# Zero rows, loads of x, clearings and the rows of h rearranged in the first epoch of a graph kernel

## The chip, the cores and the metric

The kernel runs on one core of one Trainium2 chip. The time is device microseconds of the whole launch, the median of three runs. The core has five engines with instruction queues of their own: PE (matrix multiply), DVE (vector), ACT (scalar functions), POOL (GpSimd) and SP, which here does nothing but issue DMAs. ACT and POOL issue some DMAs too. Each engine takes its instructions in program order, and an instruction that must wait holds up all those behind it on its engine.

## The reference

The input is 12,500 nodes with 128 features each and 400,000 edges. An edge e has a source node `src[e]`, a target `dst[e]` (the edges are sorted by `dst`), 20 numbers `f[e]` and a weight `w[e]`. Cut to what matters:

```python
h   = relu(layernorm(x)) @ W_in2f.T
Wij = (smu(f_ij @ W_f1.T + b_f1) @ W_f2.T + b_f2) * w[:, None]
agg = segment_sum(h[dst] * Wij, src)        # 12500 x 128
out = x + smu(agg @ W_o1.T + b_o1) @ W_o2.T + b_o2
```

`smu` is a smooth rectifier made of a linear part and an erf part. So each edge fetches a row of h by its sorted index `dst`, multiplies it by a filter that is computed from its 20 numbers, and adds the product into the row `src` of `agg`.

## The kernel before

**Tiles.** Nodes are taken in NB = 98 blocks of 128. Edges are taken in tiles of 128: four tiles make a *group* (512 edges, NG = 782 groups), and two groups make a *sup* (391 of them). Sups are divided into nine *epochs* (`PARTS`): 59 sups, or 118 groups, make the first epoch.

**What a group does.** `hide`, `bend` and `smooth` compute the hidden layer (PE `pu`, ACT `ge`, DVE `sm`); `weigh` multiplies by the second matrix (PE `pw`). `gather` fetches rows of h: a window of 128 rows of `h_dram`, loaded by `window` as `hw`, times a one-hot matrix `oh` (PE `ph`), copied by ACT to `hg`. `mix` multiplies the two (DVE `mt`, L577), `turn` transposes the product (PE `pt`), and `send` scales by the edge's weight (ACT `ms`, L597) and issues four scatters from POOL (L600), one for each tile of 128 edges. A scatter writes its 128 message rows into the DRAM buffer of the epoch, `buf`, sorted coarsely by the node block of `src`. The slot of each row is counted by `bins`, `count`, `read` and `number` (DVE `po`, `co`; PE `pc`; ACT `jk`, L495; DVE `ix`, L504). `ms` has six buffers. While epoch k is being scattered, epoch k-1's buffer is read back and summed into `agg` on PE (L655). This doesn't happen yet in the first epoch.

**SP's queue.** At the start of every second group `load(s + 3)` asks for `f`, for `rbc` (from `rel_dram`) and for the window `hw` (L405, L407, L416) of the sup three ahead. Slots of `buf` that may stay unwritten must hold zeros. `clear` writes zeros there (L167), from SP. In the first epoch the clearings of its own buffer are spread over the first 38 groups (`BY - 6`), while scatters already go to other slots of the same buffer. From group `BY` on, a scatter is ordered behind these clearings; a count taken at `BY` verifies that this was allowed. From `BY` to the end of the epoch the next epoch's buffer is cleared.

**The first epoch's other work.** The tile `agg` first holds x (as `x_sb`). `late_loads` asks for x past the first four blocks (`HEAD`) from POOL's queue (L381, L382), then for `w_sb` and small weights. `others` is a generator of small steps, which `step()` spreads evenly: it is called three times in each group and takes the next step when one is due. The steps are: for chunks c = 1 to 6 of the edge indices (512 tiles each), nine steps of `head_of(c)` (`fetched` asks for `dst` and `src` from SP, L301 and L302; `based` begins on DVE with `base_i`, L305; `written` stores `rel_dram`, L328), with the mean and variance of one block of x (`stats`, L180 and L181) after each; then the other `stats`, two blocks a step; `deviations`; and then 24 units of rows of h, each of four blocks and of six steps. The six steps of `rows_of_h` are `normed` (DVE, L191), `turned` (PE, L197), `cut` (ACT, L200), `product` (PE, L205), `first_part` (ACT L208, DVE L209) and `other_parts` (ACT L212, DVE L213, store from SP, L214). h is stored in three bf16 parts. In this order each step needs the result of the step taken just before it. `zeroed` (L731 to L733) writes zeros to the rows of `h_dram` behind the last block.

The order on PE, DVE, ACT and SP is the program's own order; there is no planner.

Of the kernel before, what the change touches and what calls it, by code (L numbers as in the profile page):

```python
# [9 lines left out]
F32 = mybir.dt.float32  # L10
# [9 lines left out]
P = 128  # L20
# [19 lines left out]
def gnn_kernel(  # L40
# [129 lines left out]


    HEAD = 4
    BY = 44
    x_sb = agg.rearrange("p (b d) -> p b d", d=D)
    mv = const.tile([P, NB, 2], F32, name="mv")
    rstd = const.tile([P, NB], F32, name="rstd")
# [84 lines left out]
    with tc.tile_pool(name="ld", bufs=4) as ld, \  # L261
# [14 lines left out]
        def fill(i):  # L276
            nc.vector.memset(fbufs[i], 1.0)

        hs = edge.tile([P, GRP, 3, D], BF, name="hs", bufs=1)
        early = eps_of[0][1] + 3  # L280

        def bank(name):
# [2 lines left out]
        def head_of(c):  # L285


            a, n = c * CH, min(CH, NT - c * CH)
            s0, m = a // SUP, (n + SUP - 1) // SUP
            rw = rowp.tile([P, ROWS, ROW], F32, name="rw").rearrange("p q r -> p (q r)")  # L290
            di, si, rel = rw[:, 0:n].bitcast(I32), rw[:, CH:CH + n].bitcast(I32), rw[:, 2 * CH:2 * CH + n]
            if c:
                rb = hs[:, :, 0, :]
            else:
                rb = edge.tile([P, SUP * P], BF, name="oh", bufs=3)[:, :CH].rearrange("p (j e) -> p j e", e=P)
            base_f = edge.tile([1, CH // SUP], F32, name="base_f")
            cells = [(j * P, min(P, n - j * P)) for j in range((n + P - 1) // P)]
            kept = [None]

            def fetched():  # L300
                nc.sync.dma_start(di, dst_col[:, a:a + n])  # L301
                nc.sync.dma_start(si, src_col[:, a:a + n])  # L302

            def based():
                nc.vector.tensor_copy(base_i[:, s0:s0 + m], di[0:1, 0:n:SUP])  # L305
                nc.vector.tensor_copy(base_f[:, :m], base_i[:, s0:s0 + m])
                nc.vector.tensor_copy(rel, di)

            def spread():
                pb = kept[0] = bank("pb")  # L310
                flat = pb.rearrange("p j e -> p (j e)")[:, :m * SUP].rearrange("p (s t) -> p s t", t=SUP)
                nc.tensor.matmul(flat, ones1, base_f[:, :m].unsqueeze(2).to_broadcast([1, m, SUP]),
                                 start=True, stop=True)

            def lowered():
                nc.vector.tensor_sub(rel, rel, kept[0].rearrange("p j e -> p (j e)")[:, :n])

            def turned():
                pd = kept[0] = bank("pd")
                for j, (o, w) in enumerate(cells):  # L320
                    nc.tensor.transpose(pd[:w, j, :], rel[:, o:o + w], ident)

            def written():
                w = cells[-1][1]
                whole = len(cells) - (w < P)
                if whole:
                    nc.scalar.activation(rb[:, :whole], kept[0][:, :whole], AF.Copy)
                    nc.sync.dma_start(rel_dram[0, a * P:(a + whole * P) * P].rearrange("(c t e) -> t c e", t=P, e=P),  # L328
                                      rb[:, :whole])
                if w < P:  # L330
                    nc.scalar.activation(rb[:w, whole], kept[0][:w, whole], AF.Copy)
                    nc.sync.dma_start(rel_dram[0, (a + whole * P) * P:(a + n) * P].rearrange("(t e) -> t e", e=P),
                                      rb[:w, whole])

            def limits():
                nc.vector.tensor_reduce(lh[:, 0, c:c + 1], rel, op=ALU.min, axis=AX.X)
                nc.vector.tensor_reduce(lh[:, 1, c:c + 1], rel, op=ALU.max, axis=AX.X)

            def bounded():
                most = edge.tile([1, 1], F32, name="most")  # L340
                nc.vector.tensor_reduce(most, base_f[:, :early], op=ALU.max, axis=AX.X)
# [22 lines left out]
        nc.scalar.dma_start(w_f2, w_f2_t)  # L364
        nc.scalar.dma_start(b2, b_f2.rearrange("o p -> p o"))
        nc.scalar.dma_start(w_sb[:, 0:CH], w_col[:, 0:CH])
        for i in range(NF):
            fill(i)
        nc.vector.memset(zero, 0.0)
# [4 lines left out]
        def late_loads():  # L374

            nc.vector.memset(x_sb[:, NB - 1, :], 0.0)
            parts_of_x = chunks(NB - 1 - HEAD, 31)
            for a, n in parts_of_x:
                nc.vector.memset(x_sb[:, HEAD + a, 0:1], 0.0)
            for a, n in parts_of_x:  # L380
                nc.gpsimd.dma_start(x_sb[:, HEAD + a:HEAD + a + n, :], bin_rows(x, HEAD + a, n))  # L381
            nc.gpsimd.dma_start(x_sb[:LASTB, NB - 1, :], x[(NB - 1) * P:N, :])  # L382
            nc.vector.memset(w_sb[:, CH:CH + 1], 0.0)
            nc.gpsimd.dma_start(w_sb[:, CH:NT], w_col[:, CH:NT])
            nc.gpsimd.dma_start(w_o1, w_o1_t)
# [309 lines left out]
            stats(edge, b)  # L695
        deviations(0, HEAD)
        rw = rowp.tile([P, ROWS, ROW], F32, name="rw")
        for step in rows_of_h(0, HEAD, *[rw[:, j * GRP:(j + 1) * GRP, 0:P] for j in range(3)], hs, bank):
            step()
        for s in range(3):  # L700
            window(s)
# [25 lines left out]
        cleared = at_first = done = 0  # L727
        work = []

        def zeroed():  # L730
            zr = edge.tile([P, 3 * D], BF, name="zr", bufs=1)  # L731
            nc.vector.memset(zr, 0.0)
            nc.sync.dma_start(h_dram[NB * P:N + WIN, :], zr[:N + WIN - NB * P, :])  # L733

        def output_bias():

            nc.vector.tensor_scalar(w_o2, w_o2, GC, None, op0=ALU.mult)
# [3 lines left out]
            nc.tensor.matmul(pb1, b1w, w_o2, start=True, stop=True)  # L741
            nc.vector.tensor_add(bo2, bo2, pb1)

        def others():
            yield one["limits"]
            yield zeroed
            left = list(range(HEAD, NB))
            for c in range(1, NC):
                it = head_of(c)
                for name in ("fetched", "based", "spread", "lowered", "turned", "written", "binned", "placed", "limits"):  # L750
                    yield it[name]
                    if left:
                        yield lambda b=left.pop(0): stats(edge, b)
            while left:
                two, left = left[:2], left[2:]
                yield lambda two=two: [stats(edge, b) for b in two]
            yield lambda: deviations(HEAD, NB)
            for b, n in chunks(NB - HEAD, GRP):
                rw = rowp.tile([P, ROWS, ROW], F32, name="rw")
                four = [rw[:, j * GRP:(j + 1) * GRP, 0:P] for j in range(3)]  # L760
                yield from rows_of_h(HEAD + b, n, *four, hs, bank)
            yield output_bias

        COUNT = 2 + 18 * (NC - 1) + (NB - HEAD - 9 * (NC - 1) + 1) // 2 + 1 + 6 * -(-(NB - HEAD) // GRP) + 1
        h_steps = others()
        taken_steps = slot = 0

        def step():

            nonlocal taken_steps, slot  # L770
            slot += 1
            while taken_steps < COUNT and taken_steps * 3 * (eps_of[0][1] * PER - 12) < slot * COUNT:
                next(h_steps)()
                taken_steps += 1

        for g in range(NG):
# [7 lines left out]
                cleared = 0  # L784
            if g < BY:

                while at_first < min(len(cleans) - 1, -(-(g + 1) * (len(cleans) - 1) // (BY - 6))):
                    apart(clear(0, at_first, nc.sync), "filled", "cleared")
                    at_first += 1
            elif k + 1 < EPOCHS:  # L790
# [34 lines left out]
            bins(g + 3)  # L825
            parts(k - 1, hi)
            step()
            assert k == 0 or taken_steps == COUNT and next(h_steps, None) is None
        k = EPOCHS - 1
        begin(k)  # L830
        choose(k, order_of[k][0])
# [222 lines left out]
```

## Time and profile before

| | |
|---|---|
| median of three runs | 4170.57 us (4166.96 to 4171.32) |
| the profiled execution | 4170.47 us, its span 4168.6 us |
| busy share of the span | PE 89%, DVE 77%, POOL 73%, ACT 68% |
| instructions | 74,614, of them 3125 scatters (L600) |
| mean granted TensorE clock | 0.97 |
| DMA traffic | 834.71 MB, 200 GB/s on average |

The profile shows one execution. A line of the table of groups gives the source line, the engine, the operation, output and input, the count, the busy time and the mean duration in ns of one, and, behind the bar, the idle time of that engine just before these instructions and which instruction ended most of it. A line of a timeline gives the start in us, the duration in us, the engine, the line and operation, and in brackets the idle time just before it and what ended that. A line of waits reads: who waited, for whom, the sum in us, how often, and the longest. A line of windows gives a stretch and its length, the busy time and count of PE, PE's weight loads, DVE, ACT and POOL, the granted clock of TensorE, the mean busy share of the 16 DMA engines, and GB/s. "SPq" is SP's DMA-issuing sequencer.

### The profile page before, as it was taken

The page shows a single profiled execution, that of the slowest core. Times are in us where ns is not written, and L with a number is a line of the kernel's source. Part 1 is how long each engine was busy: PE and PEld are TensorE (multiplying, and loading weights), DVE is VectorE, ACT ScalarE, POOL GpSimd, SP SyncE. Part 2 cuts the span into 40 slices and gives each one's busy share as a digit, 9 for nine tenths or more (in the row PEclk, how much of TensorE's full clock was granted, in tenths as well). Part 3 has the DMA queues.
Part 4 walks back from the last instruction along what each step waited for, and adds up shares of the span by engine and source line. Part 5 has one row for each costly group of instructions (what it writes and reads, how often), then busy time and mean ns, then how long its engine had stood idle before and what let it go on. Part 6 is the DMA issues. An engine that isn't in the chain of part 4 may idle for free.

```text
span 4168.6 us, 74614 instructions
## 1 busy us (share of the span) xinstructions
PE 3724.3 (89%) x18497; PEld 2310.5 (55%) x18794; DVE 3202.9 (77%) x8556; ACT 2823.1 (68%) x11054; POOL 3055.0 (73%) x3169
## 2 busy tenths in 40 slices
PE   6877888999997999979999979999899899899898
PEld 2333434655554655545655546666566566556567
DVE  6886767877776877768877768888688788788777
ACT  5776777776766777657777657777677667677651
POOL 4777767777777777777777777777777777777762
PEclk9999999999999999999999999999999999999999
DMA  8955565766656766647666747777699699788667
GB/s 232 226 149 167 175 169 177 215 202 193 201 165 190 214 203 199 199 142 217 209 202 196 200 150 216 212 212 206 180 231 232 172 250 253 211 224 223 172 186 233
DMA packets 510408, 834.71 MB, mean 200 GB/s; under 512 B 84499, under 2 KB 322852, under 8 KB 509838
## 3 DMA queue, kind: packets, MB, share of 16 engines
q1 hardware_dynamic: 393900, 608.10, 53.0%
q0 software_dynamic: 101872, 214.27, 16.7%
q10 hardware_dynamic: 14194, 7.46, 0.6%
q8 instruction: 152, 2.49, 0.3%
q14 instruction: 290, 2.38, 0.2%
HBM read 456.16 MB, written 373.36 MB: 199 GB/s over the span
## 4 chain that ended last, share of the span: by engine, by line
PE 55%; DVE 20%; DMA 14%; ACT 7%; issue 3%; POOL 1%; DVEq 0%; SPq 0%; POOLq 0%; ACTq 0%
PE pw L567 13%; PE pg L655 13%; DMA buf<-ms,ix 12%; PE pu L517 10%; PE ph L548 8%; PE pt L587 6%; DVE se L642 5%; DVE mt L577 4%; DVE sm L533 3%; ACT ge L525 2%; ACT ms L597 2%; ACT jk L495 2%; DVE co L452 1%; DVE po L438 1%; DVE agg L668 1%
## 5 line engine op out<-in xcount | busy, mean ns | idle before, releaser
L600 POOL DMA_INDIRECT buf<-ms,ix x3125 | 3013.1, 964 | 1018.3 <-issue 264.5
L655 PEld LDWEIGHTS pg<-se,rw 128*128 128x128 f32 x8036 | 1088.8, 192 | 153.0 <-issue 14.8
L597 ACT ACTIVATE ms<-pt,w_sb 128x128 f32<-128x128 f32 x3125 | 902.5, 391 | 332.5 <-PE pt L587 181.8
L655 PE MATMUL pg<-se,rw 128*128 128x128 f32 x8036 | 1110.3, 276 | 7.8 <-DVE se L642 7.8
L495 ACT ACTIVATE jk<-pc,nbig 128x98 f32<-128x98 f32 x3125 | 1024.5, 350 | 2.7 <-PE pc L466 2.0
L567 PE MATMUL pw<-sm,w_f 128*128 128x512 f32 x1564 | 885.5, 649 | 41.5 <-DVE sm L533 36.2
L525 ACT ACTIVATE ge<-pu 128x512 f32<-128x512 f32 x782 | 467.9, 598 | 569.2 <-PE pu L517 546.4
L577 DVE SCALAR_TENSOR_TENSOR mt<-pw,b,hg 128x512 f32<-128x512 f32 x782 | 583.0, 745 | 346.8 <-ACT hg L556 345.9
L517 PE MATMUL pu<-f,w_f 128*128 128x512 f32 x1564 | 814.3, 603 | 5.4 <-DVE sm L533 5.4
L587 PE MATMUL pt<-ident,mt 128*128 128x128 f32 x3125 | 494.5, 281 | 293.7 <-DVE mt L577 290.3
L533 DVE SCALAR_TENSOR_TENSOR sm<-pu,ge 128x512 f32<-128x512 f32 x782 | 535.2, 684 | 215.3 <-ACT ge L525 206.4
L642 DVE TENSOR_TENSOR se<-irow_ps,rw 128x1536 f32<-128x1536 f32 (+1 forms) x345 | 587.5, 1703 | 146.9 <-DMA rw<-buf 127.5
L556 ACT ACTIVATE hg<-ph 128x512 f32<-128x512 f32 x782 | 468.7, 599 | 325.5 <-PE ph L548 323.5
L495 ACT ACTIVATION_READ_ACCUMULATOR jk<-pc,nbig 128x1 f32 x3125 | 674.3, 216 | 0.0
L548 PE MATMUL ph<-oh,hw 128*128 128x512 bf16 (+1 forms) x2049 | 631.7, 387 | 16.6 <-issue 0.7
L587 PEld LDWEIGHTS pt<-ident,mt 128*128 128x128 f32 x3125 | 353.3, 142 | 383.4 <-DVE mt L577 375.4
L452 DVE TENSOR_TENSOR co<-co,po 128x98 f16<-128x98 f16 x2353 | 501.8, 213 | 81.1
L548 PEld LDWEIGHTS <-hw 128*128 128x128 bf16 x2346 | 233.0, 99 | 555.3 <-issue 455.9
L438 DVE TENSOR_TENSOR po<-irow_ps,hi_b 128x392 f16<-128x392 f32 x782 | 433.3, 554 | 0.0
L567 PEld LDWEIGHTS pw<-sm,w_f 128*128 128x128 f32 x1564 | 238.0, 191 | 172.8 <-DVE sm L533 163.7
L517 PEld LDWEIGHTS pu<-f,w_f 128*128 128x128 f32 x1564 | 254.3, 196 | 29.6 <-DVE sm L533 7.0
L465 PE MATMUL pc<-co,ones_h 128*128 128x392 f16 x782 | 258.0, 330 | 1.0 <-ACT ms L597 1.0
(122 smaller groups left out, 1708.6 us busy)
## 6 DMA issues: line engine op xcount, KB each, us to landing
rw<-buf SPq DMA_DIRECT2D x292, 774.0 KB
rbc<-rel_dram SPq DMA_DIRECT2D x390, 256.0 KB
buf<-zero SPq DMA_DIRECT2D x243, 387.0 KB
buf<-ms,ix POOLq DMA_INDIRECT x3125
buf<-zero SPq DMA_DIRECT2D x193, 258.0 KB
hw<-h_dram SPq DMA_DIRECT2D x391, 96.0 KB
rw<-buf SPq DMA_DIRECT2D x49, 645.0 KB
f<-in_f_t SPq DMA_DIRECT2D x390, 80.0 KB
```

Of the source, the lines that this page charges most:

```text
L495: nc.scalar.activation(jk, pc[:, j], AF.Relu, bias=nbig, accum_out=sl[:, j:j + 1])
L517: nc.tensor.matmul(pu[:, :n], w_f1, loaded[g // PER][0][:, o:o + n], start=True, stop=True)
L525: nc.scalar.activation(ge[:, :n], units_of[g][:, :n], AF.Gelu, scale=ZS)
L533: nc.vector.scalar_tensor_tensor(sm[:, :n], units_of.pop(g)[:, :n], LIN, hidden[g][:, :n], op0=ALU.mult, op1=ALU.add)
L548: nc.tensor.matmul(ph[:, :n], hw[:, q * D:(q + 1) * D], oh[:, o:o + n], start=(q == 0), stop=(q == 2))
L567: nc.tensor.matmul(pw[:, :n], w_f2, hidden.pop(g)[:, :n], start=True, stop=True)
L577: nc.vector.scalar_tensor_tensor(mt[:, :n], pws.pop(g)[:, :n], b2, rows_of.pop(g)[:, :n], op0=ALU.add, op1=ALU.mult)
L587: nc.tensor.transpose(pt[:, j, :], mt[:, j * P:(j + 1) * P], ident)
L597: nc.scalar.activation(ms[:, j, 0:P], pt[:, j], AF.Copy, scale=w_sb[:, t + j:t + j + 1])
L600: i = nc.gpsimd.indirect_dma_start(out=bufs[k][:, :], out_offset=bass.IndirectOffsetOnAxis(ap=ix[:, j:j + 1], axis=0), in_=ms[:, j, :], in ...
L642: nc.vector.tensor_tensor(se[:, :m], irow_ps.unsqueeze(1).to_broadcast([P, m, P]), rows_in[c][:, :m, P:P + 1].to_broadcast([P, m, P]), op= ...
L655: nc.tensor.matmul(pgs[0][:, g, :], rows_in[c][:, o, 0:P], sel[c][:, o, :], start=(q == 0), stop=(q == Q[k] - 1))
```

## The change

The zero rows of `h_dram` are written at the start of the kernel, from ACT's queue. x past its first four blocks is no longer asked for by POOL at once, but by SP in eight pieces of twelve blocks (the last has one DMA more for the last block): the first two right after the first `limits`, one ahead of each of chunks 2 to 6, one after them. Chunk 1 has no `stats` between its steps, so nine more blocks fall to the steps of two. The first epoch's clearings start six groups later at the same rate, and `BY` goes from 44 to 50. The rows of h are made by two units in turn: step 1 of unit A, step 1 of unit B, step 2 of A, step 2 of B, and so on. The tile `hs` gets two buffers in place of one. The generator becomes a list; it has 279 steps in place of 276.

```diff
-    BY = 44
+    BY = 50
...
-        hs = edge.tile([P, GRP, 3, D], BF, name="hs", bufs=1)
+        def parts_tile():
+            return edge.tile([P, GRP, 3, D], BF, name="hs")
...
+        zr = edge.tile([P, 3 * D], BF, name="zr", bufs=1)
+        nc.vector.memset(zr, 0.0)
+        nc.scalar.dma_start(h_dram[NB * P:N + WIN, :], zr[:N + WIN - NB * P, :])
         for i in range(NF):
             fill(i)
...
             nc.vector.memset(x_sb[:, NB - 1, :], 0.0)
-            parts_of_x = chunks(NB - 1 - HEAD, 31)
-            for a, n in parts_of_x:
-                nc.vector.memset(x_sb[:, HEAD + a, 0:1], 0.0)
-            for a, n in parts_of_x:
-                nc.gpsimd.dma_start(x_sb[:, HEAD + a:HEAD + a + n, :], bin_rows(x, HEAD + a, n))
-            nc.gpsimd.dma_start(x_sb[:LASTB, NB - 1, :], x[(NB - 1) * P:N, :])
...
-        def others():
-            yield one["limits"]
-            yield zeroed
...
-            for b, n in chunks(NB - HEAD, GRP):
...
-                yield from rows_of_h(HEAD + b, n, *four, hs, bank)
+        def named(make, names):
+            box = {}
+            def run(name, begin):
+                if begin:
+                    box.update(make())
+                box[name]()
+            return [lambda name=name, i=i: run(name, i == 0) for i, name in enumerate(names)]
+
+        def old_piece(a, n):
+            for b, m in chunks(n, n if a + n < NB else n - 1):
+                if a + b < NB - 1:
+                    nc.sync.dma_start(x_sb[:, a + b:a + b + m, :], bin_rows(x, a + b, m))
+                else:
+                    nc.sync.dma_start(x_sb[:LASTB, NB - 1, :], x[(NB - 1) * P:N, :])
+
+        def rows_unit(b, n):
+            rw = rowp.tile([P, ROWS, ROW], F32, name="rw")
+            four = [rw[:, j * GRP:(j + 1) * GRP, 0:P] for j in range(3)]
+            return dict(enumerate(rows_of_h(b, n, *four, parts_tile(), bank)))
+
+        PIECE = 12
+        loads = [lambda a=a, n=n: old_piece(HEAD + a, n) for a, n in chunks(NB - HEAD, PIECE)]
+        single = [lambda b=b: stats(edge, b) for b in range(HEAD, NB)]
+        steps = [one["limits"], loads.pop(0)]
+        for c in range(1, NC):
+            mine = named(lambda c=c: head_of(c), ("fetched", "based", ...))
+            if loads:
+                steps.append(loads.pop(0))
+            for f in mine:
+                steps.append(f)
+                if c > 1:
+                    steps.append(single.pop(0))
+        steps += loads
+        for i in range(0, len(single), 2):
+            steps.append(lambda two=single[i:i + 2]: [f() for f in two])
+        steps.append(lambda: deviations(HEAD, NB))
+        units_of_rows = [named(lambda b=b, n=n: rows_unit(HEAD + b, n), range(6)) for b, n in chunks(NB - HEAD, GRP)]
+        for i in range(0, len(units_of_rows), 2):
+            for pair in zip(*units_of_rows[i:i + 2]):
+                steps += pair
+        steps.append(output_bias)
...
-                while at_first < min(len(cleans) - 1, -(-(g + 1) * (len(cleans) - 1) // (BY - 6))):
+                while at_first < min(len(cleans) - 1, -(-(g - 5) * (len(cleans) - 1) // (BY - 12))):
                     apart(clear(0, at_first, nc.sync), "filled", "cleared")
```

More of the change, by code (lines that the diff above doesn't have):

```diff
@@ L292, in head_of @@
             if c:
-                rb = hs[:, :, 0, :]
+                rb = parts_tile()[:, :, 0, :]
             else:
@@ L697, in gnn_kernel @@
         rw = rowp.tile([P, ROWS, ROW], F32, name="rw")
-        for step in rows_of_h(0, HEAD, *[rw[:, j * GRP:(j + 1) * GRP, 0:P] for j in range(3)], hs, bank):
+        for step in rows_of_h(0, HEAD, *[rw[:, j * GRP:(j + 1) * GRP, 0:P] for j in range(3)], parts_tile(), bank):
             step()
@@ L728, in gnn_kernel @@
         work = []
[L730 to L733, printed above, removed]
         def output_bias():
@@ L742, in output_bias @@
             nc.vector.tensor_add(bo2, bo2, pb1)
-        def others():
-            yield one["limits"]
-            yield zeroed
[L747 to L757, printed above, removed]
-            for b, n in chunks(NB - HEAD, GRP):
-                rw = rowp.tile([P, ROWS, ROW], F32, name="rw")
-                four = [rw[:, j * GRP:(j + 1) * GRP, 0:P] for j in range(3)]
-                yield from rows_of_h(HEAD + b, n, *four, hs, bank)
-            yield output_bias
@@ L764, in gnn_kernel @@
-        COUNT = 2 + 18 * (NC - 1) + (NB - HEAD - 9 * (NC - 1) + 1) // 2 + 1 + 6 * -(-(NB - HEAD) // GRP) + 1
-        h_steps = others()
+        def named(make, names):
[11 more added lines that the diff above has]
+                    nc.sync.dma_start(x_sb[:LASTB, NB - 1, :], x[(NB - 1) * P:N, :])
@@ new lines, in rows_unit @@
+        def rows_unit(b, n):
[7 more added lines that the diff above has]
+        for c in range(1, NC):
+            mine = named(lambda c=c: head_of(c),
+                         ("fetched", "based", "spread", "lowered", "turned", "written", "binned", "placed", "limits"))
+            if loads:
[4 more added lines that the diff above has]
+                    steps.append(single.pop(0))
@@ new lines, in gnn_kernel @@
+        steps += loads
[7 more added lines that the diff above has]
+        steps.append(output_bias)
+        COUNT = len(steps)
@@ L772, in step @@
             while taken_steps < COUNT and taken_steps * 3 * (eps_of[0][1] * PER - 12) < slot * COUNT:
-                next(h_steps)()
+                steps[taken_steps]()
                 taken_steps += 1
@@ L827, in gnn_kernel @@
             step()
-            assert k == 0 or taken_steps == COUNT and next(h_steps, None) is None
+            assert k == 0 or taken_steps == COUNT
         k = EPOCHS - 1
```

## The prediction

> **What bounds the kernel.** I began with the page's table of groups, because the shares of busy time (PE 89%) and the chain that ended last (PE 55%, POOL 1%) disagree with what one row says.
>
> ```profile
> POOL 4777767777777777777777777777777777777762
> L600 POOL DMA_INDIRECT buf<-ms,ix x3125 | 3013.1, 964 | 1018.3 <-issue 264.5
> ```
>
> POOL runs at seven tenths nearly everywhere. 3125 scatters of 0.964 us leave 1018.3 us of idle time ahead of them. The timeline of POOL, read scatter by scatter, shows that almost all idles are exactly 0.30 us, whatever releaser is named. So 0.96 + 0.30 = 1.263 us is a scatter's pitch; a group of four takes 5.05 us. 3125 x 0.302 = 944 us of the idle time is pitch, and only 1018.3 - 944 = 74 us is waiting. The first scatter starts at 32.87, the last at 4057.54; 3124 x 1.263 = 3946 us lies between, plus about 60 us of waits and about 19 us of scatters longer than 0.96. **POOL's scatters set the time**, and the change can win only what POOL waits, wherever the other engines stand. These are its long waits in the first epoch (two ordinary scatters first):
>
> ```profile
> 35.50 0.95 POOL L600 DMA_INDIRECT buf<-ms,ix  x1 [0.30 <-ACT jk L495]
> 36.76 0.96 POOL L600 DMA_INDIRECT buf<-ms,ix  x1 [0.30 <-issue]
> 42.27 0.96 POOL L600 DMA_INDIRECT buf<-ms,ix  x1 [4.55 <-ACT hg L556]
> 49.84 0.96 POOL L600 DMA_INDIRECT buf<-ms,ix  x1 [5.34 <-DMA agg<-in_x]
> 53.65 0.96 POOL L600 DMA_INDIRECT buf<-ms,ix  x1 [2.86 <-DMA w_sb<-in_w_col]
> 58.71 0.96 POOL L600 DMA_INDIRECT buf<-ms,ix  x1 [4.11 <-DVE ix L504]
> 66.45 0.96 POOL L600 DMA_INDIRECT buf<-ms,ix  x1 [3.00 <-ACT hg L556]
> 220.67 0.96 POOL L600 DMA_INDIRECT buf<-ms,ix  x1 [2.41 <-ACT ms L597]
> 536.54 0.95 POOL L600 DMA_INDIRECT buf<-ms,ix  x1 [3.62 <-ACT hs L208]
> ```
>
> Less 0.30 each, three lots concern us. **Start:** 5.04 + 2.56 + 3.81 + 2.70 from 49.84 to 66.45, and 0.62 at 87.41: 14.7 us. (The 4.25 at 42.27 is the pipeline filling: group 1's messages are made at 40.16 in ACT's own order.) **Clearings:** 1.23 at 117.86 and 2.11 at 220.67: 3.3 us. **Rows of h:** twelve waits from 495.52 to 613.84: 11.9 us. Together 29.9 us.
>
> Why the start waits: SP's own waits, then the timelines of SP and DVE.
>
> ```profile
> SPq L733 <- DMA hw<-h_dram: 12.0, 2, 6.2
> SPq L416 <- DMA h_dram<-zr: 7.4, 1, 7.4
> ```
>
> ```profile
> 40.74 0.39 SPq L733 DMA_DIRECT2D h_dram<-zr  x1
> 41.17 0.36 SPq L301 DMA_DIRECT2D rw<-in_dst_col  x1
> ```
>
> ```profile
> 54.80 0.21 DVE L305 COPY base_i<-rw 1x64 int32<-1x64 int32 x1 [11.84 <-DMA rw<-in_dst_col]
> ```
>
> SP sits until 40.74 before the zero rows, because windows of h_dram are still being read. Chunk 1's dst is behind that on SP, is issued at 41.17, and comes at 54.8, while 7.3 MB of x and w_sb are moving. DVE stands from 42.96; group 3's messages are behind its `base_i`, and POOL waits at 58.71 and 66.45. Separately POOL itself waits at 49.84 for x and at 53.65 for w_sb: these are the 17th and 18th DMAs that it issues, x's third piece and w_sb the 9th and 10th. So I infer that each POOL DMA waits for the one eight before it to have landed.
>
> **The change, part by part.**
>
> *Zero rows first.* DVE's memset (0.22) now precedes the fills, which run without a gap into `base_i` at 7.32: +0.2 us on the path to the first scatter. ACT's issue (about 0.4) fits its hole from 6.25 to 7.44. SP loses a DMA and its 12.0 + 7.4 us of waits.
>
> *x on SP.* POOL loses four issues (0.65 + 5.24 us from 20.42), while it waits for 32.87 anyway: 0. The 8-DMA wait then meets w_sb alone, now POOL's sixth DMA, with 1.3 MB and nothing ahead of it: landed well before 43. That removes 5.04 + 2.56. SP gains nine issues of about 0.47 (its clearings' median): 4 us on a queue that stands for tens of us elsewhere. DVE drops three memsets and takes nine `stats` (about 0.42 each) out of chunk 1 into five extra double steps after the heads, where compute is far ahead of POOL: 0.
>
> *Does dst arrive?* SP reaches it at about 28.6 (window at 27.31, two pieces at 0.47), but 1.57 MB of x is ahead. From 28, x, dst and about 0.2 MB else, 2.0 MB, at the 220 to 240 GB/s of these stretches: 37, some 2 more to be seen: 39. DVE wants it at 42.96. So 3.81 + 2.70 go as well. If it is late by d, I lose d. I take 13 of the 14.7 as gained.
>
> A rule speaks against this step. The Trainium skill, DMA: Bandwidth & Descriptors, section Issuing engines are not separate DMA queues, says that DMAs of any issuing engine share the same 16 DMA engines and interleave, so that another issuer saves only issue time. By it this edit is worth POOL's 5.9 us of issue, hidden, so 0, and the bytes merely move. The trace agrees that the bytes stay, but the waits at 49.84 and 53.65 are waits of order, not of bandwidth. I side with the trace for 13 us and use the rule for the next step.
>
> *Clearings six groups later* (first at g = 6, rate unchanged, last at 43). The windows of the trace:
>
> ```profile
> 60.00:130.00 70.00, 57.98 (x195) 25.52 (x197) 57.12 (x190) 50.91 (x199) 49.92 (x52) 0.94 0.92 220
> 130.00:230.00 100.00, 82.76 (x300) 37.18 (x305) 87.74 (x299) 78.83 (x311) 74.43 (x78) 1.00 0.84 212
> ```
>
> The last two columns are DMA share and GB/s. Six of the eight pieces (4.5 MB) now fall in the 192 us of clearings: +23 GB/s on some 215, so 238, where single 10 us windows reach 243 to 262. A piece also goes just ahead of each later dst. The skill's same page (Bandwidth) prefers transfers of 1 MiB; its fit of 2.0 us + bytes/436e3 makes eight pieces 30 us and three old ones 20: an estimated 10 us more transfer time. In the trace SP waits for no landing of x between issues, so I charge nothing directly, but expect the 3.3 us of congestion waits to double: +3. Bounds: -3.3 to +15 (each of six pieces delaying scatters by most of its 786 KB / 238 GB/s = 3.3 us). The first, because the trace's bursts of three clearings and two loads cost two waits in 38 groups.
>
> Later, epoch 1's 50 clearings go into 64 groups instead of 70: 0.30 against 0.28 MB a group, at a share near 0.6: 0. Scatters from g = 50 wait for all first clearings, issued 7 groups (35 us) earlier: 0.
>
> *Rows in pairs.* Groups between 290 and 615:
>
> ```profile
> L600 POOL DMA_INDIRECT buf<-ms,ix x245 | 239.3, 977 | 86.5 <-issue 20.8 <-ACT jk L495 14.3 <-ACT ms L597 14.0
> L577 DVE SCALAR_TENSOR_TENSOR mt<-pw,b,hg 128x512 f32<-128x512 f32 x58 | 43.3, 747 | 53.2 <-ACT hg L556 53.2
> L205 PE MATMUL pg<-w_in,rw 128*128 128x128 f32 x188 | 26.6, 284 | 11.3 <-ACT rw L200 10.8
> L197 PE MATMUL pg<-ident,rw 128*128 128x128 f32 x94 | 25.7, 346 | 26.7 <-DVE rw L191 26.5
> ```
>
> In 325 us compute makes 58 groups, POOL sends 61: compute was ahead (six `ms` buffers, about 25 us usable) and eats that up by 495. Lead plus stall, 25 + 12 = 37 us over some 55 groups, is 0.67 us a group over POOL's 5.12. PE's waits at L197 and L205 are 26.7 + 11.3 = 38 us, PE being in order and the next group's matmuls behind them. In pairs each step has another unit's step between itself and its forerunner: 2 x 1.14 slots, not one. No instruction is added; the same 24 units end at the same slot (the step rate rises from 276/318 to 279/318). If only 12 of the 38 us go, the lead lasts and POOL never waits. Bounds: 0 to 11.9; I take 11. The second `hs` buffer and both `pg` banks serve two units, so neither takes the gain back.
>
> **Sum**, on the profiled span: 4168.6 + 0.2 - 13 + 3 - 11 = 4147.8; with the 1.9 us around it (4170.47 profiled, median 4170.57, the same) 4149.7. Until 2500 POOL keeps its pitch (1421 scatters in the 1800 us from 700), so the gain is carried to the end; the tail after the last scatter is untouched. I say 4149.
>
> **Rivals.** (a) Pairing moves the waits and does not shorten them: 4149 + 11 = 4160. For it: DVE and ACT are in order too, and two units' work in a row may hold `mt` and `sm`. Against: a third of the waits is enough. (b) The start's wait stays, DVE at `base_i` behind two pieces of x: the 7.6 us of POOL's own waits go, 6.5 stay, and later heads repeat it: 4149 + 10 = 4159. For: DVE waited 2.69 us for dst at 122.88 even without pieces; against: the 4 us of margin. (c) Slower: pieces and clearings together delay scatters' landings past eight pitches (10.1 us), and POOL waits at each piece. Breaking even takes 26.6 / 8 = 3.3 us a piece, the whole of its transfer; at 4.5 it gives 4170.5 - 26.6 + 36 = 4180. For: share 0.92 already; against: only 3.3 us of such waits so far. (d) Gain below what shows: (a) and (b) together, 4170.
>
> **Chances.** A run tells 0.2% (8.3 us) from nothing: below 4162.2 is faster, above 4178.9 slower. Both parts pay (4138 to 4157): 0.60. (a) 0.11, (b) 0.11, of which 0.04 end above 4162. (d) 0.08, (c) 0.10. Faster 0.78, same 0.12, slower 0.10. The range needs 8 in 10: from 4138 (all 29.9 gone would be 4140.7, and some long scatters may shorten) through (a) and (b), to 4166.
>
> **What would show it.** Right: group 3's first scatter near 52 instead of 66.45; no POOL wait on x or w_sb; `base_i` of chunk 1 without 11.84; PE's wait at L191's line in the rows of h below 13 us; no POOL wait over 1 us from 495 to 614. Wrong: long `base_i` waits behind x, or more POOL waits between 75 and 260.

## The result

| | median | lowest to highest | runs |
|---|---|---|---|
| before | 4170.94 us | 4166.12 to 4174.76 | 6 |
| after | 4153.24 us | 4147.17 to 4158.84 | 6 |

The ratio is 0.9958, with a 95% interval of 0.9946 to 0.9970: the change makes the kernel 0.42% faster, some 17.7 us. The forecast was 4149, in a range of 4138 to 4166. The profiled execution has a span of 4148.6 us, where the sum on the profiled span of before gave 4147.8.

**POOL, scatter by scatter.** Scatters from the timeline of POOL after. The first answers to the wait at 42.27, which hardly changed. The next four answer to the long waits from 49.84 to 66.45, which are gone. 104.28 and 181.49 are waits under the clearings, and 586.76 is the longest in the rows of h.

```profile
41.80 0.96 POOL L599 DMA_INDIRECT buf<-ms,ix  x1 [3.91 <-ACT hg L555]
44.45 0.96 POOL L599 DMA_INDIRECT buf<-ms,ix  x1 [0.30 <-issue]
45.71 0.96 POOL L599 DMA_INDIRECT buf<-ms,ix  x1 [0.30 <-ACT ms L596]
46.98 0.96 POOL L599 DMA_INDIRECT buf<-ms,ix  x1 [0.30 <-ACT hg L555]
52.04 0.96 POOL L599 DMA_INDIRECT buf<-ms,ix  x1 [0.30 <-issue]
104.28 0.96 POOL L599 DMA_INDIRECT buf<-ms,ix  x1 [1.51 <-issue]
181.49 0.97 POOL L599 DMA_INDIRECT buf<-ms,ix  x1 [2.19 <-ACT ms L596]
586.76 0.96 POOL L599 DMA_INDIRECT buf<-ms,ix  x1 [0.50 <-ACT hg L555]
```

Group 3 begins at 52.04 instead of 66.45. From here on "POOL's waits" are the sums of idle time ahead of each scatter less its ordinary 0.302 us, without the very first scatter. In groups 0 to 3 they fell from 18.4 to 3.6 us, in groups 11 to 49 they rose from 3.5 to 6.9, and in groups 85 to 117 they fell from 12.0 to 0.25.

**The start.** SP reaches chunk 1's dst early, and DVE finds it there. These are lines of SP's timeline and one of DVE's.

```profile
27.71 1.32 SPq L751 DMA_DIRECT2D agg<-in_x  x2
29.07 3.30 SPq L303 DMA_DIRECT2D rw<-in_dst_col  x1
```

```profile
42.42 0.34 DVE L307 COPY base_i<-rw 1x64 int32<-1x64 int32 x1
```

`base_i` has no bracket: it waited for nothing, where it waited 11.84 us before. Three later chunks did wait. This is the line of `base_i` in DVE's waits between 40 and 260 us, and its three lines in DVE's timeline:

```profile
DVE base_i L307 <- DMA rw<-in_dst_col: 11.6, 3, 5.7
102.69 0.20 DVE L307 COPY base_i<-rw 1x64 int32<-1x64 int32 x1 [5.71 <-DMA rw<-in_dst_col]
141.92 0.20 DVE L307 COPY base_i<-rw 1x64 int32<-1x64 int32 x1 [4.77 <-DMA rw<-in_dst_col]
179.81 0.20 DVE L307 COPY base_i<-rw 1x64 int32<-1x64 int32 x1 [1.08 <-DMA rw<-in_dst_col]
```

**The clearings.** The windows of after; the last two columns are DMA share and GB/s.

```profile
60.00:130.00 70.00, 55.82 (x187) 24.06 (x185) 53.91 (x182) 47.84 (x186) 52.08 (x54) 0.93 0.82 213
130.00:230.00 100.00, 80.61 (x280) 35.54 (x279) 79.54 (x268) 72.87 (x287) 72.43 (x75) 0.95 0.97 232
```

The second window went from 0.84 and 212 GB/s to 0.97 and 232. DVE did 268 instructions in it where it did 299 before, and POOL 75 where it did 78: compute fell behind by more than POOL's own waits tell.

**The rows of h.** Groups of instructions between 290 and 615, the same window as before:

```profile
L599 POOL DMA_INDIRECT buf<-ms,ix x256 | 248.0, 969 | 78.2 <-ACT jk L494 18.3 <-issue 14.0 <-ACT ms L596 14.0
L576 DVE SCALAR_TENSOR_TENSOR mt<-pw,b,hg 128x512 f32<-128x512 f32 x67 | 50.2, 749 | 34.8 <-ACT hg L555 34.7
L205 PE MATMUL pg<-w_in,rw 128*128 128x128 f32 x188 | 24.9, 275 | 0.0
L197 PE MATMUL pg<-ident,rw 128*128 128x128 f32 x94 | 18.2, 292 | 0.5 <-DVE rw L191 0.5
```

PE's waits at L205 and L197, 11.3 + 26.7 us before, went from 38.0 to 0.5 us. Compute makes 67 groups where it made 58, POOL sends 256 scatters where it sent 245, and its 78.2 us of idle time are 256 x 0.302 = 77.3 of pitch and hardly anything else.

### The profile page after: what moved, and what is told of

Its sections match the earlier page's. It is cut to its first block, busy times and chain, and to the rows that moved or that the text cites. A ratio compares the mean times of both kernels' runs of the same rounds, so it can differ in the third digit from the quotient of the medians.

```text
span 4148.6 us, 74978 instructions
## 1 busy us (share of the span) xinstructions
PE 3720.9 (90%) x18794; PEld 2304.1 (56%) x18794; DVE 3202.1 (77%) x8553; ACT 2832.9 (68%) x11054; POOL 3053.8 (74%) x3165
## 4 chain that ended last, share of the span: by engine, by line
PE 42%; DVE 12%; DMA 9%; ACT 4%; issue 2%; POOL 0%; DVEq 0%; ACTq 0%; POOLq 0%; SPq 0%
PE pg L654 11%; PE pw L566 10%; DMA buf<-ms,ix 9%; PE pu L516 7%; PE ph L547 6%; PE pt L586 5%; DVE se L641 4%; DVE mt L576 2%; DVE agg L667 1%; DVE sm L532 1%; ACT ge L524 1%; ACT ms L596 1%; PE pc L464 1%; PE pc L465 1%; ACT jk L494 1%
## 5 line engine op out<-in xcount | busy, mean ns | idle before, releaser
L547 PE MATMUL ph<-oh,hw 128*128 128x512 bf16 x2346 | 644.0, 384 | 1.7 <-DVE ix L503 1.7
```

Source lines behind the costliest of these rows:

```text
L547: nc.tensor.matmul(ph[:, :n], hw[:, q * D:(q + 1) * D], oh[:, o:o + n], start=(q == 0), stop=(q == 2))
```

## The experiments

Theory: POOL's scatters set the time; compute runs ahead of POOL by a *lead*, and POOL waits only where the lead is used up. Rivals: PE sets the time, as the chain of waits suggests; the zero rows alone made the start late; the two parts pay only together, or pairing is worth nothing once the start is early. The runs were made on several chips, on which the kernel before differs (4153 to 4156 us on three of them), so each is read by its ratio to the kernel before on its own chip. The kernel after itself was timed on one chip only.

Four of the kernels ran first on a chip on which each of them, and the kernel before, took 5260 to 5294 us; below it is called the first chip. There POOL waits 1137 to 1192 us in all (63 in the trace of before), so its ratios test little of what is told above. All four were run again on another chip, and both ratios are given.

**Does POOL set the time?** Two kernels add work to the groups of epochs 1 and 2 of the kernel after, one on POOL and one on PE. Neither alters what is computed.

```diff
+            if k in (1, 2):
+                more = cnt.tile([P, ROW], F32, name="more", bufs=2)
+                nc.gpsimd.tensor_copy(more, ms[:, 0, :])
             for j in range(n):
                 i = nc.gpsimd.indirect_dma_start(
```

> The kernel after with one copy of 128 x 129 numbers more on POOL in each of the 236 groups of epochs 1 and 2. Theory (POOL's pitch of 1.263 us a scatter sets the time): each copy adds its duration and some 0.06 to 0.3 us of pitch, 236 x 0.4 to 0.7 = 95 to 165 us, all of it in the time: 4250 to 4320. Rival (PE bounds, as the chain of work that ended last has it): under 10 us.

```diff
+            if epoch[g // PER] in (1, 2):
+                nc.tensor.matmul(pc[:, :n], ones_h, co[:, :n], start=True, stop=True)
+                nc.tensor.matmul(pc[:, :n], ones_h, co[:, :n], start=True, stop=True)
             nc.tensor.matmul(pc[:, :n], ones_h, co[:, :n], start=True, stop=False)
```

> The kernel after with two matmuls more (a repeat of the count's first, 0.17 us apart) on PE in each of the 236 groups of epochs 1 and 2. Theory (POOL sets the time; PE has 5.05 - 4.5 = 0.5 us a group to spare there): under 5 us. Rival (PE bounds): 236 x 0.34 = 80 us more, 4233.

Measured on one chip, in one set: 4178.85 us with the copies, 4130.88 us with the matmuls, 4153.53 us for the kernel before. The matmuls give 0.9944 (0.9929 to 0.9959) to the kernel before, no worse than the 0.9958 of the change without them. The copies give 1.0057 (1.0042 to 1.0073). These are the added matmuls:

```profile
L465 PE MATMUL pc<-co,ones_h 128*128 128x392 f16 x236 | 77.8, 330 | 0.0
L466 PE MATMUL pc<-co,ones_h 128*128 128x392 f16 x236 | 77.6, 329 | 0.0
```

Between the two kernels lie 48.0 us, or 0.203 us for each of 236 copies. In the traces, the scatters of epochs 1 and 2 (from the first of group 118 to the first of group 354) take 1199.1 us after, 1196.6 with the matmuls and 1243.4 with the copies, so the difference arises where the work was added. So POOL sets the time in these two epochs, and PE doesn't; for the later epochs that is carried over, not tested. The size was missed: I had expected 0.4 to 0.7 us a copy. The groups of POOL with the copies, and the scatter behind one of them, show why:

```profile
L602 POOL DMA_INDIRECT buf<-ms,ix x3125 | 3022.6, 967 | 952.6 <-issue 272.4 <-ACT jk L494 198.7 <-ACT ms L596 180.5
L600 POOL COPY more<-ms 128x129 f32<-128x129 f32 x236 | 73.3, 311 | 0.4
1000.40 1.05 POOL L602 DMA_INDIRECT buf<-ms,ix  x1 [0.16 <-issue]
```

A copy takes 0.311 us and has no idle time ahead of it, and the scatter behind it has 0.16 us instead of 0.30. So the copy fits into part of the idle time that a scatter otherwise leaves, and adds 0.2.

**Pairing alone.** The kernel before with its rows of h made by two units in turn, and two `hs` buffers.

```diff
-                yield from rows_of_h(HEAD + b, n, *four, hs, bank)
+            for i in range(0, len(blocks), 2):
+                two = []
+                for name in range(6):
+                    for u, (b, n) in enumerate(blocks[i:i + 2]):
...
+                            two[u][name]()
+                        yield made
```

> The kernel before with the rows of h made by two units in turn and nothing else. Theory (POOL's scatters set the time, and in the rows of h PE's waits at the lines of normed and cut let the other engines fall behind POOL until their lead is used up): the waits of POOL between 490 and 615 us, 11.9 us together, go, those of the start stay: 4171 - 12 = 4159. PE's waits for normed and cut fall from 38 us to under 3. Rival (the two parts only pay together, because the late start leaves too little lead): 4168 or more.

> The kernel of pairs_only again, on another chip. Theory: POOL's waits in groups 85 to 117 (12.0 us before) go to under 1; those of groups 0 to 3 (18.4) stay; 12 us or 0.3% under the kernel before on the same chip. Rival (the parts pay only together): under 0.1%.

On the first chip: 0.9948 (0.9921 to 0.9975). On the other: 4141.02 us against 4156.15, ratio 0.9965 (0.9951 to 0.9978), 15 us. POOL's waits in groups 85 to 117 are 0.08 us, those of groups 0 to 3 are 16.9. So pairing pays alone, and the rival falls. It gives 15 us where 12 were expected. The change's own ratio, 0.9946 to 0.9970 on another chip, overlaps with this interval: that the start adds to the gain of pairing is not shown by the times. The waits of the start stand in the timeline as they did:

```profile
49.75 0.96 POOL L602 DMA_INDIRECT buf<-ms,ix  x1 [4.50 <-DMA agg<-in_x]
53.56 0.95 POOL L602 DMA_INDIRECT buf<-ms,ix  x1 [2.86 <-DMA w_sb<-in_w_col]
65.18 0.96 POOL L602 DMA_INDIRECT buf<-ms,ix  x1 [2.43 <-ACT hg L558]
```

**The start alone.** The kernel after with its units one after the other.

```diff
-        for i in range(0, len(units_of_rows), 2):
-            for pair in zip(*units_of_rows[i:i + 2]):
-                steps += pair
+        for unit in units_of_rows:
+            steps += unit
```

> The kernel after, but with the units of rows of h made one after the other, as before. Theory: the gain of the start stays (14.7 us of POOL's waits), 3.4 us more are lost under the clearings, and the 12 us of waits in the rows of h come back, rather more than less since the lead is smaller (the clearings end six groups later): 4153 + 12 to 16 = 4165 to 4169. Rival (pairing is worth nothing once the start is earlier): 4153.

> The kernel of start_only again, on another chip. Theory: POOL's waits in groups 0 to 3 are about 4 us, those in groups 85 to 117 come back with 12 us or more, since compute has no greater lead at the start of the rows of h; 6 to 10 us or 0.15 to 0.25% under the kernel before on the same chip. Rival (pairing is worth nothing once the start is earlier): 0.42% under it, as the whole change.

On the first chip: 1.0021 (0.9994 to 1.0048). On the other: 4163.86 us against 4156.15, ratio 1.0019 (1.0010 to 1.0028): **slower** than the kernel before. Both theories were wrong. POOL's waits in groups 0 to 3 are 3.5 us, as forecast. But in the rows of h they are not 12 us, they are 27.7: 15.8 in groups 50 to 84, where there had been none, and 11.9 in groups 85 to 117. The timeline of POOL and the groups from 290 to 615 us in this kernel:

```profile
46.98 0.96 POOL L599 DMA_INDIRECT buf<-ms,ix  x1 [0.30 <-ACT hg L555]
422.28 1.39 POOL L599 DMA_INDIRECT buf<-ms,ix  x1 [2.36 <-ACT hs L212]
464.81 0.96 POOL L599 DMA_INDIRECT buf<-ms,ix  x1 [3.53 <-ACT jk L494]
576.65 0.96 POOL L599 DMA_INDIRECT buf<-ms,ix  x1 [2.49 <-ACT hs L208]
```

```profile
L599 POOL DMA_INDIRECT buf<-ms,ix x233 | 227.7, 977 | 98.5 <-issue 24.9 <-ACT jk L494 16.9 <-ACT ms L596 16.2
L205 PE MATMUL pg<-w_in,rw 128*128 128x128 f32 x188 | 26.7, 284 | 13.6 <-ACT rw L200 13.4
L197 PE MATMUL pg<-ident,rw 128*128 128x128 f32 x94 | 25.5, 337 | 32.2 <-DVE rw L191 32.0
```

Why, is read from the timelines of DVE and POOL together: when a group's `mt` starts, and how much later its first scatter starts (the lead). For group 50 these are the lines before, after and in this kernel:

```profile
286.68 0.74 DVE L577 SCALAR_TENSOR_TENSOR mt<-pw,b,hg 128x512 f32<-128x512 f32 x1
309.47 0.95 POOL L600 DMA_INDIRECT buf<-ms,ix  x1 [0.30 <-DVE sm L533]
285.65 0.75 DVE L576 SCALAR_TENSOR_TENSOR mt<-pw,b,hg 128x512 f32<-128x512 f32 x1
298.63 0.96 POOL L599 DMA_INDIRECT buf<-ms,ix  x1 [0.30 <-ACT jk L494]
278.76 0.74 DVE L576 SCALAR_TENSOR_TENSOR mt<-pw,b,hg 128x512 f32<-128x512 f32 x1
295.53 0.96 POOL L599 DMA_INDIRECT buf<-ms,ix  x1 [0.30 <-DMA buf<-ms,ix]
```

| kernel | `mt` of group 10 | groups 10 to 40 take | `mt` of group 50 | lead at 50 | groups 50 to 100 take |
|---|---|---|---|---|---|
| before | 93.6 us | 140.5 us | 286.7 us | 22.8 us | 285.0 us |
| zero rows alone (below) | 91.2 | 137.0 | 279.6 | 26.0 | 286.6 |
| pairing alone | 92.2 | 136.5 | 283.2 | 21.9 | 255.3 |
| start alone | 79.5 | 149.0 | 278.8 | 16.8 | 293.7 |
| after | 79.5 | 153.5 | 285.6 | 13.0 | 244.8 |

These are single traces, from several chips. Four of the kernels have the steps of before up to group 50 (one of them without the zero rows, one with the larger buffers told below), and four those of after (the two with added work among them). In the first four, groups 10 to 40 take 136.4 to 140.5 us and the lead at 50 is 21.9 to 28.0; in the others it is 146.6 to 153.5 and 13.0 to 16.8. So the differences read here are larger than the spread.

The early start puts compute 14 us ahead of before at group 10. Under the pieces of x and the clearings the next thirty groups take 8 to 13 us more (`base_i`'s waits there, 8.2 us with the start alone and 11.6 after against 2.7 before, are most of it), and at group 50 compute is only 1 to 8 us further than before. POOL is further by 11 to 14 us, so its lead is shorter by 6 to 10. The rows of h, made one unit at a time, take 5.7 to 5.9 us a group, more than POOL's 5.1. With the start alone PE's waits at the two lines are even 45.8 us instead of 38.0; why was not found. The lead is used up 27 groups earlier (the first wait is at group 59 instead of 86), and from there compute sets the pace. At group 117 the scatters stand at 666.6 us with the start alone, at 664.8 before and at 659.4 with the zero rows alone, a kernel as fast as before on a chip like this one: nothing is left of the 14 us. In pairs the rows take 4.9 to 5.1 us a group, POOL's pace, and in the traces what POOL won at the start stays won: group 117 is scattered at 640.0 us after, at 648.5 with pairing alone.

**More lead.** The kernel before with eight `ms` buffers and twelve of `ix`.

```diff
-            tc.tile_pool(name="msg", bufs=6) as msg, \
+            tc.tile_pool(name="msg", bufs=8) as msg, \
...
-            ix = cnt.tile([P, GRP], I32, name="ix", bufs=8)
+            ix = cnt.tile([P, GRP], I32, name="ix", bufs=12)
```

> The kernel before with eight buffers of messages (ms) in place of six, and twelve of ix in place of eight. Theory (compute may be ahead of POOL by as many groups as there are ms buffers; the rows of h use this lead up, and only then POOL waits): two groups, 10 us, more lead, so POOL's 11.9 us of waits in the rows of h shrink to about 2: 4171 - 10 = 4161. Rival (the waits are set by each unit's own stall, not by a lead): unchanged, 4171.

Ratio 0.9987 (0.9978 to 0.9996), 4147.91 us against 4153.53. POOL's waits in groups 85 to 117 are 7.2 us, against 10.7 in the run of the zero rows on the same chip. The sign is right and the size is half. At group 40 the lead is 25.8 us, against 26.3 in that other run, so up to there the two buffers changed nothing; at group 50 it is 28.0 against 26.0. It seems that compute reaches the bound of six buffers only near group 40 and has no time to go far beyond it.

**The zero rows alone.**

```diff
+        zr = edge.tile([P, 3 * D], BF, name="zr", bufs=1)
+        nc.vector.memset(zr, 0.0)
+        nc.scalar.dma_start(h_dram[NB * P:N + WIN, :], zr[:N + WIN - NB * P, :])
         for i in range(NF):
             fill(i)
...
-            yield zeroed
```

> The kernel before with the zero rows written at the start from ACT, and nothing else. Theory 1 (SP's 12 us stand at the zero rows makes chunk 1's dst late): dst is issued near 30 us instead of 41 and base_i waits under 3 us; POOL's waits of order for x and w_sb (7.6 us) stay: 4171 - 6 = 4165. Theory 2 (dst is late because 7.3 MB of x and w_sb share the DMA engines until 54 us): base_i still waits to about 50 or later, and the time is 4168 to 4171.

Ratio 1.0003 (0.9994 to 1.0012): nothing. The ratio alone would not settle it, since the rows of h are made one unit at a time here, and with them a larger gain of the start was lost too. The wait settles it: SP issues dst at 29.82 instead of 41.17, but it comes hardly earlier, as the timelines of SP and DVE show:

```profile
29.82 0.35 SPq L301 DMA_DIRECT2D rw<-in_dst_col  x1
52.32 0.20 DVE L305 COPY base_i<-rw 1x64 int32<-1x64 int32 x1 [9.98 <-DMA rw<-in_dst_col]
```

So SP's 12 us at the zero rows were not what made dst late. Issued 11 us earlier, it landed 2.5 us earlier. What held it shows in the DMA queues between 29.8 and 52.3 us; a line gives packets, MB, and the time of the packets as a share of the 16 engines' time. q0 holds POOL's DMAs, q1 SP's:

```profile
q0 software_dynamic: 1343, 5.96, 76.7%
q1 hardware_dynamic: 1344, 1.83, 26.6%
```

The 16 engines are full. The two queues send as many packets, but POOL's, with x and w_sb, hold three times the bytes and take three quarters of the time. So the zero rows alone bring no gain, and the gain of the start came with taking x off POOL's queue. Whether moving x is enough, with the zero rows in their old place, wasn't tried.

**Pieces behind dst.** The kernel after, each piece of x asked for after `fetched`, not before.

```diff
-            if loads:
-                steps.append(loads.pop(0))
-            for f in mine:
+            for i, f in enumerate(mine):
                 steps.append(f)
+                if i == 0 and loads:
+                    steps.append(loads.pop(0))
```

> The kernel after with each piece of x asked for behind the dst and src of the chunk that it stood ahead of. Theory (dst of chunks 3 to 5 is late because a piece of 786 KB is ahead of it in SP's queue): base_i's waits fall from 11.6 us (three) to 3 or less, POOL's waits in groups 11 to 49 from 6.9 to about 3.5: 4150. Rival (it is the clearings and the sheer bytes at a DMA share of 0.97 that make dst late): waits and time unchanged, 4153.

> The kernel of piece_after again, on another chip. Theory (a piece of x ahead of a chunk's dst in SP's queue makes base_i late, and that is why compute needs 149 to 154 us for groups 10 to 40 where the kernel before needs 141): base_i's waits between 30 and 300 us fall from 9 to 12 us to 3 or less, compute needs 140 to 145 us for groups 10 to 40, POOL's waits in groups 11 to 49 fall under 2 us; 0.1% under the whole change, so 0.50 to 0.55% under the kernel before on the same chip. Rival (the bytes of x and of the clearings together, at a DMA share of 0.97, slow that stretch, in whatever order): waits and pace as in the whole change, 0.42 to 0.56% under.

On the first chip: 0.9974 (0.9946 to 1.0002). On the other: 4130.48 us against 4154.70, ratio 0.9943 (0.9929 to 0.9956). `base_i` waits nowhere from 30 to 300 us, compute takes 136.7 us for groups 10 to 40, the lead at group 50 is 20.5 us and POOL's waits in groups 11 to 49 are 1.0. The bytes did not shrink. These are two of the chunks that waited after, and the windows:

```profile
97.41 0.20 DVE L307 COPY base_i<-rw 1x64 int32<-1x64 int32 x1
128.82 0.20 DVE L307 COPY base_i<-rw 1x64 int32<-1x64 int32 x1
60.00:130.00 70.00, 59.34 (x216) 26.00 (x214) 61.06 (x210) 55.25 (x216) 53.14 (x55) 1.00 0.89 240
130.00:230.00 100.00, 82.13 (x289) 35.94 (x288) 82.39 (x288) 74.99 (x298) 75.48 (x78) 0.97 0.98 261
```

A share of 0.98 at 261 GB/s, more than after's 232, and yet no `base_i` waits: the load alone does not make them. But the swap does two things. It takes the piece from ahead of dst, and it asks for dst one step earlier. SP's timeline for chunk 3 shows how much that is, in two lines of after and one of this kernel:

```profile
84.11 0.92 SPq L751 DMA_DIRECT2D agg<-in_x  x1
92.09 1.49 SPq L303 DMA_DIRECT2D rw<-in_dst_col  x1
84.61 1.03 SPq L303 DMA_DIRECT2D rw<-in_dst_col  x1
```

After, dst is asked for at 92.09, DVE wants it at 97.0 and has it at 102.69, 10.6 us after the issue. Asked for at 84.61 it would at that pace be there at 95.2 (an estimate), before DVE comes to it at 97.41. So the earlier issue is enough to end this wait; whether a piece just ahead also slows dst is not shown.

**Clearings early.** The kernel after with the clearings where they were before.

```diff
-    BY = 50
+    BY = 44
...
-                while at_first < min(len(cleans) - 1, -(-(g - 5) * (len(cleans) - 1) // (BY - 12))):
+                while at_first < min(len(cleans) - 1, -(-(g + 1) * (len(cleans) - 1) // (BY - 6))):
```

> The kernel after with the clearings of the first epoch where they were before (BY 44, first clearing in group 0). Theory A (the delay of the clearings keeps the first two pieces of x and chunk 1's dst from queueing behind them): base_i of chunk 1 waits again, by 2 to 5 us, POOL loses that around group 3, total 4153 + 3 = 4156. Theory B (the delay only pushes clearings onto later heads): POOL's waits in groups 11 to 49 fall from 6.9 to about 3.5, total 4150. Both may hold and cancel: 4153.

> The kernel of clear_early again, on another chip. Theory (the delay of the clearings is what lets chunk 1's dst through, but pushes the clearings' end, and with it the busy stretch, against the rows of h): with early clearings base_i of chunk 1 waits 2 to 5 us and POOL loses as much by group 4, while POOL's waits in groups 11 to 49 fall from 4 to 7 us to under 3 and compute's lead at group 50 is 18 us or more instead of 13: in all within 0.1% of the whole change, 0.35 to 0.55% under the kernel before. Rival (the delay carries the gain of the start): 0.3% or less under it.

On the first chip: 0.9984 (0.9962 to 1.0005). On the other: 4130.34 us against 4154.70, ratio 0.9941 (0.9927 to 0.9954). These are `base_i` of chunk 1 and of chunk 3, which has the longest wait:

```profile
43.58 0.27 DVE L307 COPY base_i<-rw 1x64 int32<-1x64 int32 x1 [1.24 <-DMA rw<-in_dst_col]
99.62 0.25 DVE L307 COPY base_i<-rw 1x64 int32<-1x64 int32 x1 [1.72 <-DMA rw<-in_dst_col]
```

POOL's waits in groups 0 to 3 are 4.6 us against 3.6; in groups 11 to 49 they are 1.5, compute takes 140.8 us for groups 10 to 40, and the lead at group 50 is 21.9. So the delay of the clearings isn't needed for the gain of the start, and it costs some of the lead.

The pieces of x stand ahead of dst here as they do after, and yet `base_i` waits 3.1 us in all, not 11.6. For chunk 3 dst is asked for at 90.52, 7.4 us before DVE wants it (4.9 after), and comes 9.1 us after the issue (10.6 after). So a piece ahead of dst does not by itself make the long waits either.

Both variants are clearly faster than the kernel before. Against the change itself (0.9946 to 0.9970, on another chip) their intervals overlap, so that they beat it in time is not shown. Nor do POOL's waits in groups 11 to 49 tell them apart: the four kernels with the steps of after have 1.1 to 6.9 us there. What tells them apart is the pace of groups 10 to 40 and the lead, which lie outside the spread of those four.

## Why the prediction was right, and where it was not

*The bound* holds where it was tested, in epochs 1 and 2: the kernel with more on PE lost nothing, the one with more on POOL did. It does not hold always. In the rows of h made one unit at a time compute sets the pace once its lead is gone.

*The start:* 14.7 us of waits taken away were forecast at 13, and the waits of groups 0 to 3 and of group 7 fell by 15.4. Group 3 at 52 was right to 0.04 us. That dst would beat DVE, by an estimate with 4 us of margin, was right for chunk 1. The rule of the Trainium skill (DMA: Bandwidth & Descriptors, section Issuing engines are not separate DMA queues), that DMAs of any issuer share the same 16 engines, is not against this. The trace of the zero rows agrees with it: with x on POOL's queue and dst on SP's, both took their time from the same full engines (76.7% and 26.6%). The edit did more than change the issuer: it moved most of x to a later time, and the two effects were not tested apart.

*The zero rows:* I counted no gain for SP's waits and +0.2 for the memset. The experiment agrees.

*The clearings:* "expect the 3.3 us of congestion waits to double" became 3.5 to 6.9, the forecast size, but that size is in part luck: over the traces these waits are 0.1 to 3.5 us in four kernels with the steps of before and 1.1 to 6.9 in four with those of after. The cause that I gave was wrong in part. Load alone does not explain the waits: with the pieces behind dst there were none at 261 GB/s. What the traces show is that dst was asked for too late: 4.9 us before DVE wanted it, where it took 10.6. The estimate of 10 us more transfer time used a fit that the same page (section Anatomy of one DMA) gives for DMAs issued from GpSimd, while the pieces go from SP; no run here shows it for them, and nothing in the sum rests on it.

*The rows in pairs:* 11 of 11.9 us were forecast, and POOL's waits in groups 85 to 117 fell by 11.8. The waits of PE fell from 38 to 0.5, far more than the third that was needed.

*The step that failed* is in the rivals. "Pairing moves the waits and does not shorten them: 4149 + 11 = 4160" adds two parts that do not add. Without pairing the change is slower than before: 1.0019 of 4170.94 is 4179. The mistake was to take it that "compute is far ahead of POOL" through all of the change, and to let the clearings cost only what POOL itself waits. Pieces and clearings also cost compute 8 to 13 us, hardly seen on POOL, and these are paid out of the lead. The lead at group 50 was 13 us, not the 25 on which "If only 12 of the 38 us go, the lead lasts" was built; by the same sum, 24 of the 38 had to go. With the start alone and a lead of 16.8 us, the loss was larger than the gain. It came right because pairing went far beyond the third that the prediction asked for. The chance for slower should have been tied to pairing, not to the landing of scatters.

*Carried to the end:* at group 117 the scatters were 24.8 us earlier, at the last scatter 18.4. The waits from group 118 on are alike (28.8 us before, 28.3 after), so 6 us went into pitch and durations, 5 of them into longer scatters. Groups 120 to 480 took 1825.9 us before, 1829.6 after and 1826.2 in the run with more on PE, so 3.7 of the 6 us arose there; the cause stays open. The tail behind the last scatter was 1.6 us shorter. So the nearness of the profiled 4148.6 to the sum of 4147.8 is in part luck: the first epoch gave 24.8 us where the sum has 20.8, and the loss behind it, which "the gain is carried to the end" put at nothing, made up for that.

## What to carry to other kernels

Where one engine sets the pace and the others run ahead of it through a few buffers, count the lead at each stage boundary: a stall that moves from the pacing engine to the others isn't free, it is paid when the lead runs out. A gain at the start is kept only if no later stage is slower than the pacing engine for longer than the lead lasts; so mend the slow stage first, and measure each part alone before adding their gains. A small load that an engine will soon wait for is better asked for ahead of a large one on the same queue, and early: here that swap, which asked for dst one step earlier, ended 11.6 us of waits.

## What the runs showed that I had not expected

The idle 0.30 us ahead of each scatter is not closed to other work: a POOL copy of 0.311 us between groups costs about 0.2.

On the first chip the kernel before took 5279 us (median of 35 runs, 5235 to 5316). The page of the kernel with pairing alone on that chip has these lines:

```profile
span 5277.3 us, 74683 instructions
L602 POOL DMA_INDIRECT buf<-ms,ix x3125 | 3022.6, 967 | 2118.3 <-issue 811.0
```

A scatter is as short as elsewhere (0.967 us), but POOL's idle time is twice as long, the mean granted clock is 0.902 instead of 0.97, and ACT's `ms` waits 265.9 us for something that the profile can't name. POOL waits for compute nearly everywhere there, so compute seems to set the time. Pairing alone and the start alone give the same ratios as elsewhere, but the kernel with early clearings gives 0.9984 (0.9962 to 1.0005) where it gave 0.9941 (0.9927 to 0.9954). The change itself was not timed on that chip. What slowed it was not found.
